# Cross-attention block: rows of x of batch one loaded behind batch zero's transposes, their layer norm in the first group, encoder's rows ahead of the Q products

## The chip, the cores and the metric

The kernel runs on one NeuronCore of one Trainium2 chip. The time is device microseconds of one execution. Before the change the median of three timed runs is 824.66 us (823.79 to 824.75). One more execution was recorded by the hardware profiler; all rows of the profile come from that one.

A core has five engines with queues of their own: TensorE (PE, its weight loads PEld), VectorE (DVE), ScalarE (ACT), GpSimd (POOL) and SyncE (SP), which here only issues transfers. An engine works through its instructions in the order of the program. If one waits, everything behind it waits too.

## The reference

Four batches, each with 512 rows of x and 512 rows of an encoder, 512 features, 16 heads of 32 features. All in float32.

```python
x = layer_norm(hidden_states, ln1_w, ln1_b)
q = x @ q_w + q_b ; k = enc @ k_w + k_b ; v = enc @ v_w + v_b     # 16 heads of 32
scores = einsum('bhqd,bhkd->bhqk', q, k) / sqrt(32)               # masked
out = softmax(scores) @ v
hidden = out @ cproj_w + cproj_b + hidden_states
y = layer_norm(hidden, ln2_w, ln2_b)
y = gelu(y @ fc_w + fc_b) @ proj_w + proj_b                       # 512 -> 2048 -> 512
return hidden + y
```

## The kernel before

**Groups.** The heads are worked in groups of four: 16 groups `w` = 0 to 15, four to a batch. In this text a group is named by this number. For each group there is a K product, a Q product and a V product (`prep_k`, `prep_q`, `prep_v`; lines 191 to 226): each is a chain of matmuls into one of four accumulators (`acc_tile`), which ScalarE then copies out with its bias. GpSimd adds the bias of V (`v_bias`, L230). After its last matmul each product issues the load of the same weight for two groups later (`load_w`, L189).

**Scores.** A group has four score tiles (`scores`, line 233), one for each 128 queries. TensorE writes four heads into one PSUM tile `sc`, of which there is only one: the next score tile can start when VectorE has read all four heads (L245, which also finds the row's extreme `mn`). ScalarE takes the exponential (L249). VectorE then transposes the four heads in blocks of 32 (L277) into a buffer `tb`. After two score tiles (a half, also called a pair below) it adds the reciprocals of the sums (L282 to L285), and SyncE exchanges blocks between partitions with 16 transfers (`copies`, L319) into `pT`, `gt` or `xe`. Then TensorE can multiply by V (`attend`, L362) and VectorE writes the output `oT` (L367). The very first half, of group 0, is instead transposed on TensorE (L263, with copies by VectorE L266 and ScalarE L268).

**Order.** The order is written out by hand. Every group has a list `first[w]` of work with costs, of which `run` puts a share after each score tile, so that TensorE has products between the scores. `AT` and `LAG` say after which score tile each pair is attended: the second half of group 0 before the fourth score tile of group 1, the first half of group 1 before the second score tile of group 2.

**Layer norm of x.** `inputs(b)` returns the pieces for batch `b`: `x1` loads four row tiles (`load_x`, L155), `x2` is three pieces of `ln1` (statistics of row tiles 0 and 1, L116 and L117; statistics of 2 and 3, followed by GpSimd's power `rs`, L122 and L124; normalisation of all four, L128), `x3` four turns, and `x4` loads the encoder's rows (`load_enc`, L150). A turn (`ln_turn`, line 132) transposes one slice of 128 features on TensorE and copies it out with weight and bias, on VectorE (L140) or ScalarE (L142). The turned rows `xT` and the encoder's rows `eT` of a batch lie in one buffer `xe`: the encoder's rows of batch one can be loaded only when the last K or V product of batch zero (group 3) has read those of batch zero.

**SyncE's queue.** Nearly all loads and exchanges are issued by SyncE in program order. A load whose buffer is still in use, and an exchange whose `tb` isn't finished, holds up all that is behind it. An issue also waits until the eighth transfer before it has landed.

**The start.** Loads of weights, encoder and rows of batch zero, then eight weights of the MLP, four row tiles for the residual and the output projection's weight are queued at once; then follow K and V of group 0, K of group 1, four turns, Q of group 0.

Of the kernel before, what the change touches and what calls it, by code (L numbers as in the profile page):

```python
# [74 lines left out]
def xattn_block(ctx: ExitStack, tc: tile.TileContext, x, encT, mask, q_w, k_w, v_w, c_w, fc_w, p_w, vecs, rows, out):  # L75
# [32 lines left out]
    def acc_tile(name):  # L108
        return ps_acc.tile([P, D], F32, tag="acc", name=name)
# [22 lines left out]
    def ln_turn(key, d, xn, dst):  # L132

        w, bi = (LN1W, LN1B) if key[0] == 1 else (LN2W, LN2B)
        tp = acc_tile(f"tp{key[0]}_{key[1]}_{d}")
        for t in range(NT):
            nc.tensor.transpose(tp[:, ts(t, P)], xn[t][:, ts(d, P)], ident)
        wd, bd = vec[:, w + d : w + d + 1], vec[:, bi + d : bi + d + 1]
        if d % 2:
            nc.vector.tensor_scalar(dst[:, d, :], tp, wd, bd, ALU.mult, ALU.add)  # L140
        else:
            nc.scalar.activation(dst[:, d, :], tp, AF.Identity, bias=bd, scale=wd)  # L142


    def queue(b):
        return Q[0] if b else nc.sync

    def load_enc(b):
        for d in range(ND):
            queue(b).dma_start(out=eT[:, d, :], in_=encT[b, ts(d, P), :])  # L150

    def load_x(b):
        S["xn", b] = [tiles.tile([P, D], F32, tag="xn", name=f"xn1_{b}_{t}") for t in range(NT)]
        for t in range(NT):
            queue(b).dma_start(out=S["xn", b][t], in_=x[b, ts(t, P), :])  # L155

    def ln1(b, part):

        xn = S["xn", b]
        for t in range(NT):  # L160
            if part == 2:
                ln_norm((1, b), t, xn[t], xn[t])
            elif t // 2 == part:
                ln_stat((1, b), t, xn[t])
        if part == 1:
            ln_rs((1, b))

    def ln1_turn(b, d):
        ln_turn((1, b), d, S["xn", b], xT)

    def load_mask(b, queue):
        queue.dma_start(out=m8, in_=mask[b : b + 1, :].broadcast_to([P, L]))

    def make_mb(b):
        mb = one.tile([P, L], F32, tag="mb", name=f"mb_{b}")
        nc.vector.tensor_scalar(mb, m8, 0.0, FMAX, ALU.is_equal, ALU.mult)
        if b + 1 < B:
            load_mask(b + 1, nc.gpsimd)
        S["mb", b] = mb

    def load_w(w, queue=None, names=("wk", "wq", "wv")):

        if w >= NW:
            return
        g = w % NG
        for n, src in (("wk", k_w), ("wq", q_w), ("wv", v_w)):
            if n in names:
                S[n, w] = two.tile([P, ND, P], F32, tag=n, name=f"{n}_{w}")
                (queue or Q[0]).dma_start(out=S[n, w], in_=src[:, g, :, :])  # L189

    def prep_k(w):
        b, g = divmod(w, NG)
        kT = kqp.tile([P, L], F32, tag="kT", name=f"kT_{w}")
        acc = acc_tile(f"acck_{w}")
        for d in range(ND):
            nc.tensor.matmul(acc, S["wk", w][:, d, :], eT[:, d, :], start=(d == 0), stop=(d == ND - 1))  # L196
        load_w(w + 2, names=("wk",))
        nc.scalar.activation(kT, acc, AF.Identity, bias=vec[:, KB + g : KB + g + 1], scale=1.0)
        S["kT", w] = kT

    def prep_q(w):
        b, g = divmod(w, NG)
        qT = kqp.tile([P, L], F32, tag="qT", name=f"qT_{w}")
        acc = acc_tile(f"accq_{w}")
        for d in range(ND):
            nc.tensor.matmul(acc, S["wq", w][:, d, :], xT[:, d, :], start=(d == 0), stop=(d == ND - 1))  # L206
        load_w(w + 2, names=("wq",))

        nc.scalar.activation(qT, acc, AF.Identity, bias=qb[:, g : g + 1], scale=-scale)
        S["qT", w] = qT  # L210

    def prep_v(w):
        b = w // NG
        v = five.tile([P, NT, P], F32, tag="v", name=f"v_{w}")
        acc = acc_tile(f"accv_{w}")
        for t in range(NT):
            for d in range(ND):
                nc.tensor.matmul(  # L218
                    acc[:, ts(t, P)], eT[:, d, ts(t, P)], S["wv", w][:, d, :],
                    start=(d == 0), stop=(d == ND - 1),  # L220
                )
        load_w(w + 2, names=("wv",))
        nc.scalar.copy(v, acc.rearrange("p (t f) -> p t f", t=NT))  # L223
        S["v", w] = v
        if w:
            v_bias(w)

    def v_bias(w):
        v, bias = S["v", w], row[:, 2, ts(w % NG, P)]
        nc.gpsimd.tensor_tensor(v, v, bias[:, None, :].broadcast_to([P, NT, P]), ALU.add)  # L230
# [185 lines left out]
    def norm2(b, t):  # L416
        h = S["h", b, t]
        y = tiles.tile([P, D], F32, tag="xn", name=f"xn2_{b}_{t}") if stays(b, t) else h
        S.setdefault(("yn", b), {})[t] = y
        ln_norm((2, b), t, y, h)  # L420

    def proj_bias(b):
        for t in range(NT):
            if stays(b, t):
                add_row(S["hid", b, t], 1)

    def ln2_turn(b, d):
        if d == 0:
            S["yT", b] = keep.tile([P, ND, L], F32, tag="yT", name=f"yT_{b}")
        ln_turn((2, b), d, S["yn", b], S["yT", b])  # L430
# [264 lines left out]
    CHAIN, TURN = 3.4, 0.5  # L695

    def do(fn):
        return [(0.0, fn)]

    def A(w):  # L700
        if w >= NW:
            return []
        return [
            (CHAIN, lambda: prep_k(w)),
            (CHAIN, lambda: prep_q(w)),
            (CHAIN, lambda: prep_v(w)),
        ]

    def C(b):
        return [(CHAIN, lambda t=t: cproj(b, t)) for t in range(NT)]  # L710

    def turns1(b):
        return [(TURN, lambda d=d: ln1_turn(b, d)) for d in range(ND)]

    def turns2(b):
        return [(TURN, lambda d=d: ln2_turn(b, d)) for d in range(ND)]
# [7 lines left out]
    def inputs(b):  # L724
        ln = [(0.0, lambda part=part: ln1(b, part)) for part in range(3)]
        return do(lambda: load_x(b)), ln, turns1(b), do(lambda: load_enc(b))

    def run(work, budget=None):

        spent = 0.0  # L730
        while work and (budget is None or spent + work[0][0] / 2 <= budget):
            cost, fn = work.pop(0)
            fn()
            spent += cost
        return spent
# [26 lines left out]
    prep_v(0)  # L762
    prep_k(1)
    run(turns1(0))
    make_mb(0)
    nc.vector.tensor_scalar(qb, vec[:, QB : QB + NG], 0.0, -scale, ALU.add, ALU.mult)
    prep_q(0)
# [2 lines left out]

    first = [[] for _ in range(NW)]
    later = [[] for _ in range(NW)]
    x1, x2, x3, x4 = inputs(1)
    k2, q2, v2 = A(2)
    k3, q3, v3 = A(3)
    k4, q4, v4 = A(4)
    first[0] = [(CHAIN, lambda: prep_v(1)), (CHAIN, lambda: prep_q(1))] + x1 + [k2, q2]
    first[1] = x2[:1] + [v2, k3] + x2[1:2] + [v3] + x4 + x2[2:] + [q3]
    first[2] = x3[:2] + [k4] + x3[2:] + [v4, q4] + A(5)[:1]
    first[3] = A(5)[1:] + A(6)  # L780
    mlp = []
    for p in range(NORMAL):
# [2 lines left out]
    def some(n):  # L785
        taken, mlp[:n] = mlp[:n], []
        return taken
# [10 lines left out]
    def pb_(b):  # L798
        return do(lambda: proj_bias(b))
# [7 lines left out]
    def norm(b, *ts_):  # L807
        return do(lambda: [norm2(b, t) for t in ts_])


    x1, x2, x3, x4 = inputs(2)
    first[3] = x1 + first[3] + cb(0)
    k, q, v = A(7)
    c, t2 = C(0), turns2(0)
    first[4] = [k] + x2[:1] + [q] + x2[1:2] + [v] + x4 + x2[2:]
    later[4] = c[:1] + x3[:2] + c[1:2] + x3[2:] + c[2:] + stat(0, 0, 1, 2, 3) + rs(0)
    k, q, v = A(8)
    first[5] = norm(0, 0, 1, 2, 3) + [q, k] + t2[:2] + [v] + t2[2:] + pb_(0) + some(5)
    k, q, v = A(9)
    x1, x2, x3, x4 = inputs(3)  # L820
    first[6] = [k, q] + some(5) + [v] + x1
    k, q, v = A(10)
    first[7] = [k, q] + x2[:1] + some(3) + x2[1:2] + some(3) + [v]

    k, q, v = A(11)
    first[8] = h_(1, 0, 1) + x2[2:] + [k, q] + x3[:2] + some(1) + x3[2:] + [v] + h_(1, 2, 3) + x4
    later[8] = cb(1) + C(1)
    k, q, v = A(12)
    first[9] = [q] + some(2) + [k] + some(3) + [v]
    k, q, v = A(13)  # L830
    first[10] = [k, q] + some(5) + [v]
    k, q, v = A(14)
    t2 = turns2(1)
# [3 lines left out]
    k, q, v = A(15)  # L837
# [99 lines left out]
```

## Time and profile before

| what | value |
|---|---|
| median of three timed runs | 824.66 us (823.79 to 824.75) |
| profiled execution | 822.63 us |
| its span, first to last instruction | 820.5 us |
| around the span | 2.1 us |
| TensorE busy | 803.1 us, 98% |
| VectorE busy | 563.1 us, 69% |
| ScalarE busy | 348.0 us, 42% |
| GpSimd busy | 90.6 us, 11% |
| mean granted TensorE clock | 0.998 |

Each row of a timeline gives the start and the length in us, the engine, the line of the program, the operation, what it writes and reads, and in brackets how long the engine sat idle before it and what released it. Consecutive instructions of one kind are merged and counted (x8). TensorE does a float32 matmul in two passes, so a chain of four shows as x8. The stretches give, for windows of the span, how long each engine was busy, the granted TensorE clock (1.00 is full), the share of DMA engines in use and GB/s. "To landing" is the time from the start of a transfer's issue until its data has landed.

### The profile page before, as it was taken

To read this page: it belongs to the slowest core of one execution; us is meant where nothing else is said; L and a number is where in the kernel's file an instruction comes from. 1 tells how busy PE (TensorE), PEld (TensorE's weight loads), DVE (VectorE), ACT (ScalarE), POOL (GpSimd) and SP (SyncE) were. 2 spreads that over 40 slices of the span, in tenths; PEclk is the share of its full clock that TensorE was granted. 3 is DMA by queue.
4 is the path that set the end of the run, shared out by engine and by line. 5 is a ranking of instruction groups with operands and counts; after the bars stand their busy time and mean duration, and the time that the engine had idled before them with its cause. 6 is when DMAs were issued, how large, how long until landed. Compare 5 with 4: busy or idle time off the path is not lost.

```text
span 820.5 us, 11894 instructions
## 1 busy us (share of the span) xinstructions
PE 803.1 (98%) x4020; PEld 465.9 (57%) x4020; DVE 563.1 (69%) x1264; ACT 348.0 (42%) x741; POOL 90.6 (11%) x98
## 2 busy tenths in 40 slices
PE   9996999999999999999999999999999999999998
PEld 6552545444454554454544444444447888888887
DVE  3698889986576778667886767787327986368511
ACT  2655555356654744465436367556202331023200
POOL 1001003111000111000111210010201012200011
PEclk9999999999999999999999999999999999999999
DMA  9668789756668768678677676877734550023001
GB/s 328 235 150 241 184 240 252 191 148 161 168 160 231 179 169 238 159 207 200 155 205 190 164 194 159 199 174 184 205 116 166 191 169 14 26 78 90 2 13 39
DMA packets 59740, 134.91 MB, mean 164 GB/s; under 512 B 12144, under 2 KB 14320, under 8 KB 59552
## 3 DMA queue, kind: packets, MB, share of 16 engines
q1 hardware_dynamic: 58416, 130.73, 58.8%
q0 software_dynamic: 736, 2.29, 0.8%
q10 hardware_dynamic: 528, 1.14, 0.6%
q8 instruction: 32, 0.52, 0.3%
q14 instruction: 28, 0.23, 0.1%
HBM read 58.74 MB, written 6.29 MB: 79 GB/s over the span
## 4 chain that ended last, share of the span: by engine, by line
PE 91%; DVE 5%; SPq 2%; DMA 1%; issue 1%; ACT 0%; POOL 0%; DVEq 0%; POOLq 0%; ACTq 0%
PE accp L467 14%; PE accf L457 14%; PE q L561 12%; PE sc L240 8%; PE av L362 7%; PE accc L399 6%; PE acck L196 6%; PE accv L218 6%; PE accq L206 6%; DVE s L245 2%; PE q4p L601 2%; PE q3p L601 2%; PE q7p L601 2%; PE q6p L601 2%; PE q2p L601 2%; PE q1p L601 2%
## 5 line engine op out<-in xcount | busy, mean ns | idle before, releaser
L249 ACT ACTIVATE s<-s,mn 128x512 f32<-128x512 f32 x256 | 181.6, 711 | 139.6 <-DVE mn L245 139.3
L245 DVE CUSTOM_DVE_ANT_0 s<-sc,mb 128x512 f32<-128x512 f32 x256 | 161.3, 686 | 53.8 <-PE sc L240 53.7
L277 DVE STREAM_TRANSPOSE tb<-s 128x512 f32<-128x512 f32 x248 | 161.6, 690 | 8.5 <-ACT s L249 8.5
L457 PE MATMUL accf<-yT,fcw 128*128 128x512 f32 x256 | 115.5, 599 | 1.5 <-DVE yT L140 1.5
L467 PE MATMUL accp<-pw,gt 128*128 128x512 f32 x256 | 115.0, 598 | 0.0
L457 PEld LDWEIGHTS accf<-yT,fcw 128*128 128x128 f32 x256 | 47.2, 190 | 66.5 <-issue 55.9
L467 PEld LDWEIGHTS accp<-pw,gt 128*128 128x128 f32 x256 | 47.2, 190 | 63.8 <-issue 61.1
L240 PE MATMUL sc<-kT,qT 32*128 32x512 f32 x512 | 73.0, 640 | 4.6 <-DVE mn L245 3.8
L218 PEld LDWEIGHTS accv<-wv,xe 128*128 128x128 f32 x512 | 58.7, 192 | 9.0 <-issue 6.5
L196 PE MATMUL acck<-xe,wk 128*128 128x512 f32 x128 | 60.3, 615 | 3.2 <-DMA xe<-encT_dram 3.2
L218 PE MATMUL accv<-wv,xe 128*128 128x128 f32 x512 | 60.8, 277 | 0.7 <-ACT xe L142 0.4
L561 PE MATMUL q<-ys,gt 128*128 128x256 f32 x256 | 60.1, 379 | 0.0
L206 PE MATMUL accq<-xe,wq 128*128 128x512 f32 x128 | 58.5, 600 | 0.0
L399 PE MATMUL accc<-wc,oT 128*128 128x512 f32 x128 | 56.9, 597 | 0.0
L362 PE MATMUL av<-pT,v 128*32 128x256 f32 x864 | 52.2, 382 | 1.7 <-DMA wv<-v_w_dram 1.7
L561 PEld LDWEIGHTS q<-ys,gt 128*128 128x128 f32 x256 | 48.6, 190 | 6.6
L249 ACT ACT_TABLE_LOAD x22 | 28.2, 1283 | 52.7 <-DVE mn L245 52.7
L230 POOL TENSOR_TENSOR v<-v,row 128x512 f32<-128x512 f32 x16 | 20.3, 1270 | 264.3 <-ACT v L223 264.3
L249 ACT ACTIVATION_READ_ACCUMULATOR s<-s,mn 128x1 f32 x256 | 47.8, 187 | 0.0
L561 PE MATMUL q<-yT,gt 128*128 128x256 f32 x192 | 46.3, 379 | 0.0
L196 PEld LDWEIGHTS acck<-xe,wk 128*128 128x128 f32 x128 | 23.8, 195 | 36.0 <-issue 31.2
L362 PEld LDWEIGHTS av<-pT,v 128*32 128x32 f32 x864 | 25.5, 109 | 30.3 <-issue 11.9
(117 smaller groups left out, 841.5 us busy)
## 6 DMA issues: line engine op xcount, KB each, us to landing
pT<-tb SPq DMA_DIRECT2D x416, 136.0 KB, 2.4
fcw<-fc_w_dram SPq DMA_DIRECT2D x32, 256.0 KB, 3.1
pw<-p_w_dram SPq DMA_DIRECT2D x32, 256.0 KB, 3.5
gt<-fc_w_dram SPq DMA_DIRECT2D x32, 256.0 KB, 2.8
gt<-tb SPq DMA_DIRECT2D x48, 136.0 KB, 2.4
wk<-k_w_dram SPq DMA_DIRECT2D x16, 256.0 KB, 3.4
xe<-encT_dram SPq DMA_DIRECT2D x16, 256.0 KB, 5.2
wv<-v_w_dram SPq DMA_DIRECT2D x16, 256.0 KB, 3.2
```

The costliest lines, as they stand in the source:

```text
L196: nc.tensor.matmul(acc, S["wk", w][:, d, :], eT[:, d, :], start=(d == 0), stop=(d == ND - 1))
L206: nc.tensor.matmul(acc, S["wq", w][:, d, :], xT[:, d, :], start=(d == 0), stop=(d == ND - 1))
L218: nc.tensor.matmul(acc[:, ts(t, P)], eT[:, d, ts(t, P)], S["wv", w][:, d, :], start=(d == 0), stop=(d == ND - 1),)
L240: nc.tensor.matmul(sc[:, h, :], qT[r, ts(qt, P)], kT[r, :], start=True, stop=True)
L245: nc.vector.tensor_tensor_reduce(out=s, in0=sc[:, h, :], in1=S["mb", w // NG], scale=1.0, scalar=FMAX, op0=ALU.add, op1=ALU.min, accum_out=mn,
L249: nc.scalar.activation(s, s, AF.Exp, bias=mn, scale=-1.0, accum_out=sums[:, qt, h : h + 1])
L277: nc.vector.transpose(tv[:, q, h], S["ps", w, qt][h])
L362: nc.tensor.matmul(av[ts(h, HD), : 2 * P].rearrange(shape, **kw), v[:, t, ts(h, HD)], p[t][h], start=(t == 0), stop=(t == NT - 1),)
L399: nc.tensor.matmul(acc, S["oT", b][:, g, ts(t, P)], wc[:, g, :], start=(g == 0), stop=(g == NG - 1))
L457: nc.tensor.matmul(acc, S["fcw", b, f][:, d, :], S["yT", b][:, d, :], start=(d == 0), stop=(d == ND - 1))
L467: nc.tensor.matmul(acc, gT[q % 2][:, k, ts(t, P)], S["pw", b, q * FQ + k], start=(k == 0), stop=(k == FQ - 1))
L561: nc.tensor.matmul(o, a[:, k], y[:, k], start=(k == 0), stop=(k == 1))
```

## The change

Four things are moved, and nothing is computed that wasn't computed before.

- The four row tiles of x of batch one are loaded right behind the turns of batch zero, ahead of the Q product of group 0, no longer in the middle of group 0.
- The layer norm of batch one, three pieces, is placed into group 0 (before: the statistics in group 1, the normalisation before the last product of group 1). Two of its turns come at the end of group 1 instead of the beginning of group 2.
- The products of groups 1 to 3 are put in another order: K of group 3 and V of group 2 move into group 0, Q of group 2 into group 1. V of group 3 is the first product of group 1, and the load of the encoder's rows of batch one is issued right behind it, ahead of Q of groups 2 and 3. Before, it was issued behind V of group 3 too, but later in group 1.
- In every `ln_turn`, of both layer norms and all batches, slices 1 and 2 are copied by VectorE and slices 0 and 3 by ScalarE; before, 1 and 3 by VectorE, 0 and 2 by ScalarE. In group 5 three turns instead of two stand before the V product.

```diff
@@ ln_turn @@
-        if d % 2:
+        if d in (1, 2):
             nc.vector.tensor_scalar(dst[:, d, :], tp, wd, bd, ALU.mult, ALU.add)
         else:
             nc.scalar.activation(dst[:, d, :], tp, AF.Identity, bias=bd, scale=wd)
@@ the start @@
     run(turns1(0))
+    x1, x2, x3, x4 = inputs(1)
+    run(x1)
     make_mb(0)
...
     prep_q(0)
...
-    x1, x2, x3, x4 = inputs(1)
...
-    first[0] = [(CHAIN, lambda: prep_v(1)), (CHAIN, lambda: prep_q(1))] + x1 + [k2, q2]
-    first[1] = x2[:1] + [v2, k3] + x2[1:2] + [v3] + x4 + x2[2:] + [q3]
-    first[2] = x3[:2] + [k4] + x3[2:] + [v4, q4] + A(5)[:1]
+    first[0] = [(CHAIN, lambda: prep_v(1))] + x2[:1] + [(CHAIN, lambda: prep_q(1))] + x2[1:2] + [k2] + x2[2:] + [k3, v2]
+    first[1] = [(CHAIN, lambda: (prep_v(3), load_enc(1)))] + [q2, q3] + x3[:2]
+    first[2] = [k4] + x3[2:] + [v4, q4] + A(5)[:1]
...
-    first[5] = norm(0, 0, 1, 2, 3) + [q, k] + t2[:2] + [v] + t2[2:] + pb_(0) + some(5)
+    first[5] = norm(0, 0, 1, 2, 3) + [q, k] + t2[:3] + [v] + t2[3:] + pb_(0) + some(5)
```

The instructions of the two kernels are the same in number and kind. On VectorE the first two statistics stand right behind the two copies of the first transposed score tile, the other two behind the reciprocals of that half, and the normalisation between the transposes of the third score tile and the reading of the fourth. On TensorE the K products of groups 2 and 3 stand before the third and fourth score tile of group 0.

## The prediction

> **What bounds the kernel now.** TensorE is busy 803.1 of 820.5 us, so a change can win only what TensorE waits for or runs at a lowered clock. I read first the waits of TensorE (who waited for whom: total us, times, longest):
>
> ```profile
> PE sc L240 <- DVE mn L245: 3.8, 3, 2.7
> PE acck L196 <- DMA xe<-encT_dram: 3.2, 1, 3.2
> PE av L362 <- DMA wv<-v_w_dram: 1.7, 1, 1.7
> PE accf L457 <- DVE yT L140: 1.5, 1, 1.5
> ```
>
> The first two, 7.0 us, lie close together. The timeline of TensorE (start, length, idle before and its releaser) puts them in groups 1 and 2:
>
> ```profile
> 56.53 1.14 PE L240 MATMUL sc<-kT,qT 32*128 32x512 f32 x8 [0.60 <-DVE mn L245]
> 61.37 1.93 PE L362 MATMUL av<-pT,v 128*32 128x256 f32 x32
> 63.83 1.14 PE L240 MATMUL sc<-kT,qT 32*128 32x512 f32 x8 [0.52 <-DVE mn L245]
> 71.26 1.14 PE L240 MATMUL sc<-kT,qT 32*128 32x512 f32 x8 [2.66 <-DVE mn L245]
> 76.66 5.36 PE L196 MATMUL acck<-xe,wk 128*128 128x512 f32 x8 [3.23 <-DMA xe<-encT_dram]
> ```
>
> The last row also takes 5.36 us where other K products take 3.70. The stretches of 1 us say why (columns: stretch, its length, five busy times, granted clock, DMA share, GB/s):
>
> ```profile
> 72.00:73.00 1.00, 1.00 (x10) 0.67 (x7) 1.00 (x3) 0.97 (x3) 0.00 (x0) 1.00 0.73 235
> 75.00:76.00 1.00, 0.00 (x0) 0.00 (x0) 1.00 (x5) 0.82 (x3) 0.00 (x0) 1.00 0.81 289
> 78.00:79.00 1.00, 1.00 (x2) 0.34 (x1) 1.00 (x3) 0.78 (x3) 0.00 (x0) 0.50 1.02 278
> 80.00:81.00 1.00, 1.00 (x4) 0.39 (x3) 0.02 (x1) 0.00 (x0) 0.00 (x0) 0.97 1.00 244
> ```
>
> After the 3.2 us wait the clock is 0.50 from about 76.6 to 80.0. So some 8.7 us are at stake between 56 and 82: 7.0 of waiting and 1.7 of clock. VectorE is the engine behind group 1: it runs from 47.5 to 80 without a pause, layer norm included:
>
> ```profile
> 29.71 0.69 DVE L245 CUSTOM_DVE_ANT_0 s<-sc,mb 128x512 f32<-128x512 f32 x1 [0.52 <-PE sc L240]
> 52.40 0.65 DVE L116 BATCH_NORM_STATS2 st<-xn 128x6 f32<-128x512 f32 x1
> 66.10 2.33 DVE L128 TENSOR_SCALAR xn<-xn,mv,rs 128x512 f32<-128x512 f32 x4
> ```
>
> Last, SyncE's queue. One exchange of a pair is 16 issues in 10.4 us, and all wait in one line with the loads:
>
> ```profile
> 22.23 1.00 SPq L189 DMA_DIRECT2D wq<-q_w_dram  x1
> 33.61 1.81 SPq L155 DMA_DIRECT2D xn<-x_dram  x4
> 46.80 10.43 SPq L319 DMA_DIRECT2D pT<-tb  x16
> 72.13 1.85 SPq L150 DMA_DIRECT2D xe<-encT_dram  x4
> ```
>
> **The change, step by step.** I walk the new order with durations of before, on its clock. A score tile costs VectorE 2.45 us (four L245), its transposes 2.41, the end of a half (L282 to L285) 0.97; TensorE takes 1.07 for scores, 3.63 for a K or Q product, 3.77 for V, 1.86 for an attend.
>
> *1. Rows of x.* The four loads move from 33.6 to the place of the Q weight issued at 22.2, past three weight loads (Q of group 2, V and Q of group 3); these come later but are wanted only at about 51 to 70. The place is in the start-up backlog, with 390 GB/s moving. For the Q weight in that place the trace shows
>
> ```profile
> L189 SPq DMA_DIRECT2D wq<-q_w_dram x1: 997/997/997, 22.2 to 22.2; - x1
> DMA to landing us min/median/max: 8.4/8.4/8.4
> ```
>
> that is 22.2 + 8.4 = 30.6. The loads before it land at 28.7, 29.4 and 30.0 (8.5, 8.5, 8.4 after issue), 0.65 apart, so I put the rows at 30.6, 31.3, 31.9, 32.6. The Trainium skill (DMA: Bandwidth & Descriptors, section on the anatomy of one DMA) fits 2.0 us plus bytes over 436 GB/s, stated for the GpSimd path: 256 KB give 2.6 us and a landing near 25, before VectorE asks. I take the row: it is this queue, loaded. By the rule the sum below would be about 1.4 us better.
>
> *2. Statistics in group 0.* VectorE is free at 29.2, but L116 of row tiles 0 and 1 stand ahead of the next four L245. They wait for the landings, end at about 32.15, and L245 starts there instead of at 29.71: 2.4 late. Behind it are the exponentials (ScalarE ends 35.7 instead of 33.3), then the copy of Q (36.3), whose accumulator the fourth transpose needs, then ScalarE's copy of the first transpose (36.9), whose accumulator the next K product needs. That product starts at 36.95 instead of about 34.9: TensorE loses 2.0.
>
> *3. Two K products ahead of scores.* K of group 2 now stands before the third score tile and K of group 3 before the fourth. Scores end at 41.7; VectorE starts them at 41.8 instead of 36.05. Statistics 2 and 3 (1.58) and GpSimd's power (1.5) fit in before. Then 2.45 + 2.41 to 46.65, the four L128 (1.85, no GpSimd beside them) to 48.5, 2.42 + 2.40 + 0.97 to 54.3, plus 0.3 because L284 falls beside GpSimd's V bias: 54.6. Before, this half was done at 46.8.
>
> *4. Its exchange* therefore runs 54.65 to 65.1 and lands at 64.5 + 2.4 = 66.9 (2.4 us is the row of the last issues). Before it landed at 59.0 and the attend at 61.37 did not wait.
>
> *5. TensorE in between.* K 40.6, scores 41.7, K 45.3, scores 46.4, V 50.1, row sums and attend 52.2, scores 53.3, V 57.0; scores wait for VectorE until 57.5 and end 58.6; Q 62.2; scores 63.45. Then the attend waits for the exchange: 3.45 us. It ends 68.8, scores 69.85, Q 73.5, two turns 74.5, scores 75.6.
>
> *6. The encoder.* Its issues follow the exchange and two V weights: 66.0 to 67.9, landing 70.4 to 73.1 (4.4 to 5.7 after issue). K of group 4 asks at 75.6 and doesn't wait: the 3.2 us and their clock are gone. But the next exchange starts 1.9 later for it: 67.9 to 78.3, landed 80.2. TensorE has done K and a turn at 79.7, waits 0.5, attends to 82.1, scores 83.2, turn 83.7, V 87.35.
>
> *7. The sum.* That V product ended at 89.55 before: 2.2 us gained. From here both orders are alike, TensorE has no idle time until 141, and later exchanges land 0.9 or more before their attends, so the gain stays.
>
> *8. The clock.* The new wait of 3.45 us can halve the clock too. The Trainium skill (TensorE: Matmul & The Clock Gate, Part 1) says the clock halves after a whole idle window of 3.4 us, windows running free. A 3.45 us wait hardly ever holds a whole one, so by the rule nothing is lost. The rows above are stricter: 3.2 us were enough, while 2.66 us just before were not. I take the row: 1.7 lost, of which the 0.5 wait of step 6 is absorbed, so 1.2. Gain left: 1.0.
>
> *9. Turns.* Feature slices 1 and 2 go to VectorE, 0 and 3 to ScalarE, all through: no instruction more. In batch zero the Q product reaches slice 2 at 19.2, after VectorE's second turn (18.4). In batch two and three the copies land beside waits of another cause. These I cost at 0, hidden by TensorE's queue of products; without cover each is at most 0.8, one L140. In group 5, though, the wait at L457 (1.5) ends on VectorE, where
>
> ```profile
> 182.31 1.21 DVE L284 COPY rr<-rsum 128x256 f32<-128x256 f32 x1
> ```
>
> takes 1.21 instead of 0.29, ending just after GpSimd's V bias (182.10 to 183.36). A third turn now stands before that V product (0.44), so the bias starts near 182.55 and L284 may be through at 182.60: 0.9 gained. If it is caught all the same, 0.4 lost. I take 0.9.
>
> Sum: 1.0 + 0.9 = 1.9 us off the profiled execution's 822.63 (820.5 span and 2.1 around it), 820.7. The timed median is 824.66, 2.0 above it; I take the difference over: 822.8.
>
> **The rivals.** *A, the cover holds.* The rows land before 29.2, or the clock stays. Without the wait of step 2 VectorE reaches 40.4 instead of 41.8 and the whole walk is 0.9 to 1.4 better; with the clock kept, 1.2 more. For it: the free-running window. Against: 390 GB/s in the rows up to 28. Time: 824.66 - 4.0 = 820.6.
> *B, slower: the exchange of step 4 takes the place of the waits removed.* Everything that delays VectorE between 30 and 54 goes one for one through the exchange into the attend at 63.45. For it: before, that attend had 2.4 us to spare, and now it has less than none. The 1.9 us are used up when it lands after 68.8, 1.9 later than I have it. Rows of x landing 1.9 later do it; at 3.9 later the time is 822.8 + 3.9 = 826.7.
> *C, no change.* The clock is halved and L284 is caught: 1.0 - 0.4 = 0.6 gained, 824.1.
>
> **How the numbers follow.** Mine 0.45, A 0.17, B 0.23, C 0.15. Within 0.2%, 1.65 us, a measurement of this kernel can't tell a change. Mine lies at 1.9 with an uncertainty of about 1.2, so 0.29 of its 0.45 are faster and 0.16 the same; A is faster; B slower by more than 1.65 in 0.20; C the same. Faster 0.47, same 0.33, slower 0.20. The range goes from a little under A, 820.2, to B at 826.7.
>
> **What would show it.** Right: no wait of L196 for the encoder near 75; a wait of about 3.5 us of L362 for an exchange near 63 to 67, with the clock at 0.50 for some 3 us behind it; L116 waiting for x until about 30.6 and 31.3; 2 us lost in short waits from 33 to 37; L284 near 182 at 0.29. Wrong: rows of x that land at 26 or after 33; the attend not waiting; a wait after 90 that before didn't have.

## The result and the profile after

The changed kernel took 824.97 us (median of 12 runs, 822.91 to 827.83), the kernel before in the same series 824.93 us (12 runs, 823.79 to 828.24): ratio 0.9995, 95% interval 0.9981 to 1.0009, so between 1.6 us faster and 0.7 us slower. The forecast of 1.9 us gained did not come; no change is what was measured. The profiled execution took 823.17 us with a span of 821.4.

The waits of TensorE in the changed kernel (who waited for whom: total us, times, longest):

```profile
PE av L362 <- DMA pT<-tb: 6.7, 2, 3.4
PE accv L218 <- ACT xe L142: 0.9, 1, 0.9
PE accv L218 <- ACT yT L142: 0.9, 1, 0.9
PE av L362 <- DMA gt<-tb: 0.4, 1, 0.4
PE accf L457 <- DVE yT L140: 0.2, 1, 0.2
```

The waits that headed the list before are gone: 3.8 us for VectorE before scores, 3.2 for the encoder, 1.5 at L457. In their place stand two waits, 3.3 and 3.4 us, of an attend for its exchange. The timeline of TensorE shows where:

```profile
57.47 1.14 PE L240 MATMUL sc<-kT,qT 32*128 32x512 f32 x8 [0.30 <-DVE mn L245]
66.78 3.64 PE L362 MATMUL av<-pT,v 128*32 128x256 f32 x32 [3.34 <-DMA pT<-tb]
70.35 1.96 PE L240 MATMUL sc<-kT,qT 32*128 32x512 f32 x8
77.81 3.70 PE L196 MATMUL acck<-xe,wk 128*128 128x512 f32 x8
82.39 1.93 PE L362 MATMUL av<-gt,v 128*32 128x256 f32 x32 [0.45 <-DMA gt<-tb]
145.31 1.93 PE L362 MATMUL av<-pT,v 128*32 128x256 f32 x32 [3.40 <-DMA pT<-tb]
```

The K product of group 4 (77.81) no longer waits for the encoder and takes its normal 3.70. The attend of pair 1 (66.78) waits 3.34 us, and it and the scores behind it run at half speed: 3.64 in place of 1.93, 1.96 in place of 1.14. Stretches of 3.41 us of the changed kernel (stretch, length, five busy times with TensorE's first, granted clock, DMA share, GB/s) show the clock at half from 65.2 to 72.0:

```profile
61.80:65.22 3.42, 1.58 (x10) 0.31 (x8) 3.35 (x9) 2.20 (x7) 0.00 (x0) 1.00 0.97 222
65.22:68.63 3.41, 1.85 (x20) 1.07 (x24) 3.41 (x11) 2.41 (x7) 0.00 (x0) 0.50 0.85 247
68.63:72.04 3.41, 3.41 (x28) 1.02 (x20) 2.15 (x4) 0.51 (x2) 0.00 (x0) 0.50 1.02 343
```

The attend of pair 7 (145.31) is the second loser. Before, it stood like this:

```profile
143.65 1.93 PE L362 MATMUL av<-pT,v 128*32 128x256 f32 x32 [1.75 <-DMA wv<-v_w_dram]
```

Where does one execution stand against the other? The first K product took 4.52 us after and 3.60 before, and the first transposes of batch zero began at 16.71 against 15.68. The change has nothing ahead of them; in the runs below that product takes between 3.60 and 4.73, so it goes with the execution. The table gives both readings, by the time in the span and counted from those transposes (us that the changed kernel is ahead):

| at | in the span | from the transposes |
|---|---|---|
| V product of group 4 ends | 0.0 | 1.0 |
| V product before pair 7's attend starts | 0.0 | 1.0 |
| pair 7's attend starts | -1.7 | -0.6 |
| scores at 157 | -0.7 | 0.3 |
| attend at 187, behind L457 | 0.2 | 1.2 |
| last product | -0.9 | 0.1 |

Up to pair 1's exchange the first reading is the better one, since the walk there hangs on the landing of x, which does not move with TensorE's start: in two runs below the transposes began 1.28 and 0.92 us earlier than here, and pair 1's exchange only 0.38 and 0.21. So nothing was won by 90, 1.7 us were lost at 145, 0.9 came back by 157 (transposes and a wait for L400 that no longer lie in the way), 0.9 at L457, and 1.1 went in two waits of the V product for ScalarE's turns, near 299 and 429. Single executions of either kernel differ by 4 to 5 us, so that these two end 0.9 apart goes with equal medians.

### The profile page after: what moved, and what is told of

Its sections match the earlier page's. It is cut to its first block, busy times and chain, and to the rows that moved or that the text cites. A ratio compares the mean times of both kernels' runs of the same rounds, so it can differ in the third digit from the quotient of the medians.

```text
span 821.4 us, 11900 instructions
## 1 busy us (share of the span) xinstructions
PE 805.0 (98%) x4020; PEld 467.0 (57%) x4020; DVE 562.7 (69%) x1264; ACT 347.7 (42%) x741; POOL 90.4 (11%) x98
## 3 DMA queue, kind: packets, MB, share of 16 engines
q10 hardware_dynamic: 528, 1.14, 0.5%
## 4 chain that ended last, share of the span: by engine, by line
PE 85%; DMA 5%; DVE 5%; SPq 3%; issue 1%; ACT 1%; DVEq 0%; ACTq 0%
PE accp L467 14%; PE accf L457 14%; PE q L561 12%; PE sc L240 7%; PE accc L399 7%; PE av L362 6%; PE accv L218 4%; PE acck L196 4%; PE accq L206 4%; SPq L319 3%; PE q4p L601 2%; PE q3p L601 2%; PE q7p L601 2%; PE q2p L601 2%; PE q5p L601 2%; PE q6p L601 2%
## 5 line engine op out<-in xcount | busy, mean ns | idle before, releaser
L245 DVE CUSTOM_DVE_ANT_0 s<-sc,mb 128x512 f32<-128x512 f32 x256 | 161.3, 686 | 55.4 <-PE sc L240 55.2
L457 PE MATMUL accf<-yT,fcw 128*128 128x512 f32 x256 | 115.5, 599 | 0.5 <-ACT v L223 0.3
L457 PEld LDWEIGHTS accf<-yT,fcw 128*128 128x128 f32 x256 | 47.2, 190 | 65.5 <-issue 55.5
L362 PE MATMUL av<-pT,v 128*32 128x256 f32 x864 | 53.9, 391 | 6.7 <-DMA pT<-tb 6.7
L367 DVE TENSOR_TENSOR oT<-av,pT 128x256 f32<-128x256 f32 x26 | 11.0, 422 | 46.7 <-PE av L362 43.9
```

Source lines behind the costliest of these rows:

```text
L245: nc.vector.tensor_tensor_reduce(out=s, in0=sc[:, h, :], in1=S["mb", w // NG], scale=1.0, scalar=FMAX, op0=ALU.add, op1=ALU.min, accum_out=mn,
L362: nc.tensor.matmul(av[ts(h, HD), : 2 * P].rearrange(shape, **kw), v[:, t, ts(h, HD)], p[t][h], start=(t == 0), stop=(t == NT - 1),)
L457: nc.tensor.matmul(acc, S["fcw", b, f][:, d, :], S["yT", b][:, d, :], start=(d == 0), stop=(d == ND - 1))
```

## The experiments

**The two halves of the change.** First the mapping of the turns alone, on the kernel before:

```
-        if d % 2:
+        if d in (1, 2):
...
-    first[5] = norm(0, 0, 1, 2, 3) + [q, k] + t2[:2] + [v] + t2[2:] + pb_(0) + some(5)
+    first[5] = norm(0, 0, 1, 2, 3) + [q, k] + t2[:3] + [v] + t2[3:] + pb_(0) + some(5)
```

> The kernel before with the eviction mapping of the transposes (slices 1 and 2 on VectorE) and the third turn of group 5 alone; all loads and products as before. Theory T (the late exchange of pair 1, the halved clock behind it and the backlog of SyncE that reaches pair 7 ate the gain): the mapping is worth nearly nothing, 1.1 us gained at L457 in group 5 (wait 1.54 becomes 0.3 to 0.5), 0.4 lost at the V product near 299 and 0.65 at the one near 429: within 0.3 us of the kernel before; attend of pair 1 and of pair 7 wait as before (0 and 1.7). Rival M (the mapping ate the gain): at least 1 us slower than the kernel before.

823.92 us against 824.01: ratio 0.9998 (0.9982 to 1.0015). The three places came out as expected; from TensorE's waits in this kernel:

```profile
PE av L362 <- DMA wv<-v_w_dram: 2.8, 1, 2.8
PE accv L218 <- ACT xe L142: 0.9, 1, 0.9
PE accv L218 <- ACT yT L142: 0.9, 1, 0.9
PE accf L457 <- DVE yT L140: 0.2, 1, 0.2
```

The gain at L457 and the losses at the two V products cancel. Pair 7 waited 2.8 us here, against 1.75 before, though nothing ahead of it but the mapping had changed; whether the mapping or the execution made that 1.0 us is open.

Then the moves alone: the changed kernel with both edits above undone.

> The changed kernel with the mapping of the kernel before (slices 1 and 3 on VectorE, two turns ahead of V in group 5). T: pair 1's attend still waits 3.3 us and is halved in clock for 6 us or more, pair 7's still waits 3.4; L457 in group 5 waits 1.5 again, V products near 299 and 429 wait 0.4 and 0.2: within 0.3 us of the changed kernel. M: at least 1 us faster than the changed kernel.

825.45 us: ratio 1.0014 (0.9997 to 1.0031), no difference from the kernel before or the changed one that the interval can settle. The waits are as expected: 1.5 at L457, and

```profile
66.38 3.38 PE L362 MATMUL av<-pT,v 128*32 128x256 f32 x32 [3.33 <-DMA pT<-tb]
69.69 1.14 PE L240 MATMUL sc<-kT,qT 32*128 32x512 f32 x8
145.83 3.64 PE L362 MATMUL av<-pT,v 128*32 128x256 f32 x32 [3.77 <-DMA wv<-v_w_dram]
```

Pair 1's attend waits as in the changed kernel (3.33 and 3.34), but here half speed ends with it, after 3.4 us and not 6 or more: 1.45 us lost instead of 2.5. At pair 7 it is the other way round. So half speed behind the same wait costs differently; why, the part on step 8 shows.

**Pair 1's exchange.** Is it late because VectorE's work stands ahead of it? The normalisation of batch one's rows was moved out of the way:

```
-    first[0] = ... + x2[1:2] + [k2] + x2[2:] + [k3, v2]
-    first[1] = [(CHAIN, lambda: (prep_v(3), load_enc(1)))] + [q2, q3] + x3[:2]
+    first[0] = ... + x2[1:2] + [k2, k3, v2]
+    first[1] = [(CHAIN, lambda: (prep_v(3), load_enc(1)))] + x2[2:] + [q2, q3] + x3[:2]
```

> The changed kernel with the normalisation of batch one's rows (four L90) moved from behind K of group 2 in group 0 to behind V of group 3 in group 1. T: VectorE reaches the second score tiles 1.2 to 1.8 us earlier, pair 1's exchange lands near 65.0, its attend waits 1.5 to 2.1; clock gate either not tripped (then 3.5 to 4 us ahead at the V product of group 4) or as in the changed kernel (1.5 ahead). Q products of group 1 must not wait for the later transposes by over 1 us. Rival X: no change.

824.08 us: ratio 0.9999 (0.9984 to 1.0014). (The normalisation is the four L128; L90 in the expectation is a slip.) The exchange began at 52.61, 2.07 us earlier than in the changed kernel, TensorE came 0.77 earlier, and the attend waited 1.22 less, 2.12 us: what VectorE saves here comes off TensorE's wait one for one, less the 0.77. Rival X, that nothing changes there, falls. But the saving was spent at once, in TensorE's timeline of this run:

```profile
64.78 2.86 PE L362 MATMUL av<-pT,v 128*32 128x256 f32 x32 [2.12 <-DMA pT<-tb]
68.16 2.09 PE L240 MATMUL sc<-kT,qT 32*128 32x512 f32 x8 [0.51 <-DVE mn L245]
70.18 4.82 PE L206 MATMUL accq<-xe,wq 128*128 128x512 f32 x8
144.39 3.47 PE L362 MATMUL av<-pT,v 128*32 128x256 f32 x32 [3.52 <-DMA wv<-v_w_dram]
```

Three operations at half speed cost 0.9, 0.95 and 1.1 us, more than behind the longer wait. Pair 7's attend began 0.9 us earlier than in the changed kernel and lost 1.5 of it again by half speed.

The V product of group 2 was taken out of VectorE's and TensorE's way as well, in two versions. In the first it landed behind the load of batch one's encoder rows, so V of group 2 is there computed from batch one's rows and not from batch zero's:

```
-    first[0] = ... + [k3, v2]
-    first[1] = [(CHAIN, lambda: (prep_v(3), load_enc(1)))] + [q2, q3] + x3[:2]
+    first[0] = ... + [k3]
+    first[1] = [(CHAIN, lambda: (prep_v(3), load_enc(1)))] + [v2, q2, q3] + x3[:2]
```

> The changed kernel with one product moved: V of group 2 goes from the end of group 0 to the start of group 1. Two K products then still stand ahead of the third score tile's turn, but not the V product. T: pair 1's half is done near 52.5 in place of 54.7, its exchange has landed near 64.9, TensorE asks for it near 65: wait under 0.5 us, no slice at half clock, V product of group 4 ends near 85 to 86 (89.5 in the changed kernel). What of these 4 us reaches the end depends on pair 7: if its exchange stays where it is, its wait grows from 3.4 to 5 or more and the gain at the end is 1 to 2 us; if it moves along, 3 to 4 us. Rival X (the landing of x at 30.6 and VectorE behind it set the loss): no change.

835.21 us, ratio 1.0133 (1.0100 to 1.0166). It says nothing on either theory: the V product waited 12.2 us for the encoder rows. The second version puts it ahead of that load:

```
+    first[1] = [v2] + [(CHAIN, lambda: (prep_v(3), load_enc(1)))] + [q2, q3] + x3[:2]
```

> The changed kernel with V of group 2 moved from the end of group 0 to the start of group 1, ahead of V of group 3 and of the load of batch one's encoder rows. Theory T: pair 1's half is done 2.5 us earlier, its exchange has landed when TensorE asks for it (wait under 0.7 us, no half clock there), and 4 us are gained at the first product behind it; but SyncE's queue, full from pair 1's exchange to pair 7's, only moves up by these 2.5 us, so pair 7's attend waits longer than the 3.4 us of the changed kernel, 4.5 to 5.5, and 2 to 3 us are gained at the end. Rival V (VectorE's work, not the queue, sets pair 7): pair 7 waits as before, 4 us gained at the end.

828.37 us, ratio 1.0037 (1.0023 to 1.0052): slower. From TensorE's timeline:

```profile
64.85 1.93 PE L362 MATMUL av<-pT,v 128*32 128x256 f32 x32
78.64 6.54 PE L196 MATMUL acck<-xe,wk 128*128 128x512 f32 x8 [5.21 <-DMA xe<-encT_dram]
```

Pair 1's attend waits for nothing and keeps its clock, as expected. But the encoder's issues, which follow V of group 3, now come behind the second exchange in SyncE's line, at 74.92 instead of 65.96, and the K product waits 5.21 us and runs at half speed for 2.8 more. The wait that the change had removed is back, larger. At pair 1 T's mechanism held; its sum did not, because this queue was left out of it. At pair 7 T and V both missed: the attend waited 2.58 us, neither 4.5 to 5.5 nor the 3.40 of the changed kernel.

**Pair 7: queue or transfers?** My theory was that SyncE's queue, full of issues from pair 1's exchange on, keeps pair 7's exchange back. In the changed kernel VectorE finished pair 7's half at 129.7, and SyncE started its exchange at 132.72:

```profile
115.28 1.87 SPq L155 DMA_DIRECT2D xn<-x_dram  x4
117.73 13.28 SPq L319 DMA_DIRECT2D gt<-tb  x16
132.72 10.29 SPq L319 DMA_DIRECT2D pT<-tb  x16
```

So the weights' issues were given to another engine, first to GpSimd:

```
-                (queue or Q[0]).dma_start(out=S[n, w], in_=src[:, g, :, :])
+                (queue or (nc.gpsimd if 2 <= w < 10 else Q[0])).dma_start(out=S[n, w], in_=src[:, g, :, :])
```

> The changed kernel with the loads of the K, Q and V weights of groups 2 to 9 issued by GpSimd instead of SyncE: 12 issues with their gaps, some 6.7 us, leave SyncE's queue between pair 1's exchange and pair 7's. T (the queue is full there and sets pair 7): pair 7's exchange starts 4 to 6 us earlier, its attend waits under 0.5 us, 3.4 to 5 us gained over the changed kernel; pair 1's wait of 3.3 stays. Rival V: pair 7's wait stays above 2.5 us and the time within 0.5 us of the changed kernel.

> The kernel before with the same weights issued by GpSimd. T: pair 7's attend, which waited 1.75 us in the profile before and 2.7 in that of the mapping alone, waits under 0.5: 1.5 to 3.5 us faster than before, and less gain than the same edit brings on the changed kernel. Rival V: within 0.5 us of before.

> Both: V of group 2 first in group 1, and the weights of groups 2 to 9 issued by GpSimd. T: neither pair 1 nor pair 7 makes TensorE wait over 0.7 us: 6 to 8 us faster than the changed kernel and than the kernel before. If the gains of the two edits do not add, 3 to 5.

832.23, 829.12 and 836.05 us: ratios 1.0097 (1.0077 to 1.0117), 1.0050 (1.0034 to 1.0066) and 1.0141 (1.0122 to 1.0160). All slower, all expectations missed. VectorE and GpSimd of the changed kernel with this edit show where most of it goes; the other two kernels have the same copy at 5.81 us:

```profile
129.92 1.27 POOL L230 TENSOR_TENSOR v<-v,row 128x512 f32<-128x512 f32 x1
130.42 5.81 DVE L284 COPY rr<-rsum 128x256 f32<-128x256 f32 x1
131.15 4.93 POOL L374 TENSOR_TENSOR h<-h,row 128x512 f32<-128x512 f32 x4
```

A copy that takes 0.29 us alone ended only when GpSimd had ended its V bias and four additions behind it; then pair 7's half was 5 us late. Without the edit the same copy took 0.82, ending with the V bias (it came 0.60 us after the bias began, here 0.50). To test that cause, the four additions were moved behind the next mask's load, which waits for VectorE:

```
-    first[3] = x1 + first[3] + cb(0)
+    first[3] = x1 + first[3]
...
-    first[4] = [k] + x2[:1] + ...
+    first[4] = cb(0) + [k] + x2[:1] + ...
```

> The changed kernel with the weights issued by GpSimd as in the earlier run, and the four additions of the projection's bias to batch zero's rows (L374, 4.9 us on GpSimd) moved from the end of group 3 to the start of group 4, behind the mask's load, where no copy L284 of VectorE meets them. Theory G (the copy L284, held 5.81 us while GpSimd ran its V bias and these additions, was the loss of the earlier run): L284 takes under 1.5 us everywhere, pair 7's half is done 4.5 us earlier, its wait falls from 7.2 to under 3, 5 to 8 us faster than the earlier run. Rival: GpSimd's own issues or the order of the weights were the loss: no more than 1 us faster.

827.32 us, ratio 1.0027 (1.0017 to 1.0038), against 1.0097: 5.8 us faster by the ratios. G holds: L284 took 0.94 and pair 7's wait fell from 7.2 to 3.15, a little short of the "under 3". That this kernel is still 0.27% slower than the one before is not accounted for. What is left answers the question: here SyncE starts pair 7's exchange as soon as VectorE has written its half, and yet TensorE waits 3.15 us.

```profile
132.45 0.94 DVE L284 COPY rr<-rsum 128x256 f32<-128x256 f32 x1
133.93 10.05 SPq L319 DMA_DIRECT2D pT<-tb  x16
149.09 3.64 PE L362 MATMUL av<-pT,v 128*32 128x256 f32 x32 [3.15 <-DMA xe<-encT_dram]
```

The last issue ends at 144.0 and the attend begins 5.1 us later; in the changed kernel 2.3 us later. The queue was free and the transfers were late, though here with loads from GpSimd among them.

The same with ScalarE as the issuer, so that GpSimd is left alone, each load behind the eviction of its product:

```
-        load_w(w + 2, names=("wk",))
         nc.scalar.activation(kT, acc, ...)
+        load_w(w + 2, names=("wk",))
```

> The changed kernel with the weights of groups 2 to 9 issued by ScalarE, each behind the eviction of its own product, so that GpSimd keeps its work and its order (the copy L284 of pair 7's second half took 0.82 us behind the V bias in the changed kernel, and 5.81 us with GpSimd's issues). T (SyncE's queue, full from pair 1's exchange on, sets pair 7): pair 7's exchange starts at VectorE's end near 130 in place of 132.7, its attend waits under 1.2 us instead of 3.4 and loses no clock: 2 to 4 us faster than the changed kernel. Pair 1's wait of 3.3 stays. Rival D (the transfers themselves, not their issue, are what is slow there: the DMA engines were 0.9 busy from 96 to 146): pair 7's wait stays above 2.5 and the time within 1 us of the changed kernel.

> The kernel before with the same edit. T: no K product waits over 2 us for the encoder rows (3.2 before, the two weights ahead of them gone), pair 7's attend waits under 1.2 us: 2 to 5 us faster than before. Rival D: within 1 us of before.

846.12 and 848.28 us: ratios 1.0251 (1.0235 to 1.0267) and 1.0282 (1.0268 to 1.0295). T is refuted: taking the issues off SyncE made both kernels 20 us slower. D said that moving issues gains nothing, but did not foresee a loss. It shows in the exchanges, here two of the changed kernel with the edit:

```profile
86.47 13.17 SPq L319 DMA_DIRECT2D pT<-tb  x16
99.74 12.98 SPq L319 DMA_DIRECT2D gt<-tb  x16
```

With loads in ScalarE's queue as well, the 16 issues of an exchange take 13 to 17 us where they took 10 to 13.3 (only the first, ahead of most of these loads, still takes 10.1 in the changed kernel). Why, these runs do not tell: the DMA engines were busy only 0.7 to 0.8 of most of that time.

Last, bytes and issues both taken away. The weights of groups 4 to 7 are not loaded; these groups multiply by those of groups 2 and 3:

```
             if n in names and 4 <= w < 8:
                 S[n, w] = S[n, w - 2]
             elif n in names:
```

> The changed kernel without the loads of the K, Q and V weights of groups 4 to 7: these groups multiply by the weights of groups 2 and 3 that lie in the two buffers. This leaves out 12 transfers of 256 KB (3 MB), ten of them between pair 1's exchange and pair 7's, and with them both their bytes and their issue on SyncE; every instruction on TensorE, VectorE and ScalarE stays. Theory D, after the runs that moved the issue and gained nothing (the stretch from 55 to 145 is full of transfers, the DMA engines 0.9 busy, and pair 7 comes as late as they are through): each exchange starts when VectorE has written its half, pair 7's near 129.7, it lands within 2.5 us of its last issue, its attend waits under 0.8 us in place of 3.4: 3 to 5 us faster than the changed kernel. Pair 1's wait of 3.3 stays. Rival V (VectorE's half of pair 7 comes too late for TensorE whatever the transfers do): pair 7's wait stays above 2 us, gain under 1.5 us.

821.48 us against 825.33: ratio 0.9954 (0.9940 to 0.9967), 3.8 us faster than the kernel before, from which the changed kernel doesn't differ. Rows of SyncE, then of TensorE, lines counted two higher here because of the edit:

```profile
114.14 11.03 SPq L321 DMA_DIRECT2D gt<-tb  x16
128.09 10.07 SPq L321 DMA_DIRECT2D pT<-tb  x16
```

```profile
66.49 3.41 PE L364 MATMUL av<-pT,v 128*32 128x256 f32 x32 [3.27 <-DMA pT<-tb]
141.55 1.93 PE L364 MATMUL av<-pT,v 128*32 128x256 f32 x32 [1.34 <-ACT v L225]
```

Pair 1 waits 3.27 as without this edit; two of the 12 loads stood ahead of it, and they do not make it late. Pair 7 waits 1.34 instead of 3.40, and the 0.45 of the attend near 82 is gone. (The profile names ScalarE's copy as the releaser, but it had ended at 140.9; the last issue of the exchange, at 137.54, took 3.8 us to land, to 141.4.) Rival V falls on both of its numbers. D's bound of 0.8 was too low: the exchange starts when VectorE has written its half (128.03), but its last issue landed after 3.8 us where D counted on 2.5. Of the 3.4 us some 2.1 go with these 12 loads. How much is their issue and how much their bytes, this run can't tell: both were taken away.

## Why the prediction was right and wrong

*Steps 1 to 5 held almost to the tenth, step 6 in part.* In the rows of VectorE and SyncE of the changed kernel:

```profile
30.60 0.69 DVE L116 BATCH_NORM_STATS2 st<-xn 128x6 f32<-128x512 f32 x1 [0.38 <-DMA xn<-x_dram]
32.24 0.69 DVE L245 CUSTOM_DVE_ANT_0 s<-sc,mb 128x512 f32<-128x512 f32 x1
54.68 10.12 SPq L319 DMA_DIRECT2D pT<-tb  x16
65.96 2.14 SPq L150 DMA_DIRECT2D xe<-encT_dram  x4
68.22 12.27 SPq L319 DMA_DIRECT2D gt<-tb  x16
```

Forecast were 30.6 for the rows, 32.15 for L245, 54.65 for the exchange, 66.0 for the encoder, waits of 3.45 and 0.5 for the two attends; measured 3.34 and 0.45. That the 0.45 came out is luck. The exchange behind the encoder took 12.27 us where step 6 counted 10.4, since two of the encoder's loads took 6.8 and 7.1 us to land and not 5.7 at most; it landed at 82.3 and not at 80.2, and TensorE came about as much later. The row of the loaded queue was right about the landing, the 2.0 us plus bytes of the page cited there was not. TensorE's start 1.0 us later took nothing from this: it shortened VectorE's wait for x by as much.

*Step 7 failed: "later exchanges land 0.9 or more before their attends, so the gain stays".* The trace before shows at 143.65 an attend that already waited 1.75 us for its exchange, and the first fence of the prediction lists it; a gain ahead of it would have needed an earlier exchange. It became a later one. VectorE had written the half at 129.7 in both profiles; the exchange began at 130.70 before and at 132.72 after. From the moment VectorE had written that half, the runs show:

| run | us to the attend | of these, until the exchange began |
|---|---|---|
| kernel before | 13.9 | 1.0 |
| mapping alone | 14.9 | 1.2 |
| changed kernel | 15.6 | 3.0 |
| moves alone | 16.0 | 3.2 |
| normalisation later | 15.7 | 2.5 |
| V of group 2 behind the encoder's load | 14.0 | 1.5 |
| V of group 2 first in group 1 | 14.8 | 2.3 |
| without weights of groups 4 to 7 | 13.5 | 0.1 |

With the moves and all loads on SyncE the exchange begins 1.5 to 3.2 us behind VectorE, without the moves 1.0 and 1.2. The stretches of 10 us of the kernel before (DMA share second to last):

```profile
86.00:96.00 10.00, 10.00 (x80) 6.04 (x79) 9.93 (x26) 7.50 (x19) 1.27 (x1) 1.00 0.54 139
116.00:126.00 10.00, 10.00 (x80) 5.47 (x73) 8.00 (x22) 5.74 (x15) 0.00 (x0) 1.00 0.98 288
```

and of the changed kernel:

```profile
46.00:56.00 10.00, 10.00 (x105) 7.74 (x98) 9.86 (x25) 3.80 (x11) 1.27 (x1) 1.00 0.10 30
86.00:96.00 10.00, 10.00 (x80) 6.06 (x79) 9.93 (x25) 6.74 (x17) 1.26 (x1) 1.00 0.91 234
116.00:126.00 10.00, 10.00 (x80) 5.45 (x73) 7.99 (x22) 5.73 (x15) 0.00 (x0) 1.00 0.90 252
```

Before, the exchange of pair 1 ran from 46.8, and there was slack near 90. In the changed kernel next to nothing moves until 54.7, and from then on the share is 0.86 to 0.96 up to 146. It looks as if the pause of step 4 were missing as transfer time 80 us later, but SyncE's rows of these two profiles do not bear that out: the exchange ahead of pair 7's began at 117.72 in the kernel before and at 117.73 in the changed one, so its queue had made the pause up by then. Nor has the mapping alone a pause, and it has 1.0 of the 1.7 us. The 2.0 us arose inside that exchange (13.28 us where it took 11.28), and they begin with one load of x ahead of it, the third of batch two's four, issued at 116.2 in both kernels. From its issue to its landing, in the kernel before and in the changed one:

```profile
DMA to landing us min/median/max: 4.3/4.3/4.3
DMA to landing us min/median/max: 6.4/6.4/6.4
```

It landed at 122.60, and an issue waits until the eighth transfer before it has landed: the exchange's sixth issue began at 122.62, after a gap of 1.8 us, and the next two at 123.86 and 125.25, as the two loads behind it landed at 123.85 and 125.24. With the moves alone that load took 5.4 us, and there the exchange itself began 1.7 us later, at 119.43. So three things stand: the attend of pair 7 waited before already, the load traffic of groups 4 to 7 is some 2.1 of its 3.4 us, and in these single executions the moves go with a later exchange there. By what the moves delay it, and how much of the 1.7 us was that one execution, is open.

*Step 8 was right that the clock halves, and mis-sized: 1.7 us lost in the forecast, of which 0.5 were to be absorbed by the next attend's wait, 2.5 in the profile with 0.45 of that wait left.* TensorE came to the next attend at 81.94, some 0.5 later than the forecast had it with its 1.7; and because the exchange landed late as well, the 0.45 came on top. Together they are the 1.0 us which step 8 had still left and the profile has not. More telling is the spread. Behind waits at the same attend:

| run | wait | half speed | lost to it |
|---|---|---|---|
| changed kernel | 3.34 | 65.2 to 72.0 | 2.5 |
| moves alone | 3.33 | 66.0 to 69.4 | 1.45 |
| without weights of groups 4 to 7 | 3.27 | 66.8 to 70.2 | 1.6 |
| normalisation later | 2.12 | 65.6 to 72.5 | 3.0 |

Half speed lasts 3.41 us or a multiple of it, and what is lost is about half of the time TensorE works in it. And the 2.66 us wait for VectorE that cost nothing in the kernel before cost 1.5 us with the mapping alone. In steps of 3.41 us, laid so that the changes of the clock fall on their borders, the kernel before (first two rows) and the mapping alone (last two) show why:

```profile
66.40:69.81 3.41, 2.20 (x6) 0.65 (x4) 3.41 (x8) 0.35 (x1) 0.38 (x1) 1.00 0.94 217
69.81:73.23 3.42, 1.97 (x16) 1.17 (x16) 3.42 (x10) 3.16 (x9) 0.00 (x0) 1.00 0.89 231
68.60:72.01 3.41, 1.01 (x3) 0.18 (x1) 3.41 (x10) 1.54 (x5) 0.00 (x0) 1.00 0.93 215
72.01:75.42 3.41, 3.15 (x14) 1.65 (x15) 3.34 (x9) 1.97 (x5) 0.00 (x0) 0.50 0.86 239
```

Before, the wait fell on two steps, with TensorE idle for 1.2 and 1.45 us, and nothing followed. With the mapping alone one step had 2.4 us idle, and the next ran at half speed. All fourteen traces agree (counted from 20 us on): of the steps at full speed, all 26 with 2.1 us or more idle were followed by half speed, none of some 3200 with 1.7 or less; of the 7 in between, 3 were. A step at half speed was followed by another when TensorE was idle for 0.9 us or more of it, and never at 0.4 or less. In the changed kernel the end of the wait lay in such a step (1.56 us idle, second row of its stretches above), and so a second one followed; with the moves alone it was 0.4. So the price of a wait hangs on where it falls in these steps, which the walk could not know: that it was 2.5 here and not 1.45 is chance. The page weighed there (TensorE: Matmul & The Clock Gate, Part 1) has windows of that length, running free, and these rows agree; its whole idle window is not needed, 2.12 us of 3.41 were enough.

*Step 9:* the 0.9 at L457 came (1.54 became 0.29 and 0.19). The zero for batches two and three was wrong by 0.44 and 0.65 us at the V products near 299 and 429, where slice 3 is now ScalarE's and ends later; the bound of 0.8 each, given there, holds.

*The sum*, from the profile, in the span: 0.0 up to the V product of group 4 (forecast 1.0), -1.7 at pair 7 (0), +0.9 behind it (0), +0.9 at L457 (0.9), -1.1 at the turns (0): -1.0, and -0.9 is read at the end (forecast 1.9). That 824.97 lies in the range of 820.2 to 826.7 is owed to the width of the range: a gain of 1.0 by 90 was forecast and none was there. Of the rivals, no change came out, but not by its mechanism: L284 near 182 was not caught. B's mechanism is there, nearly one for one with the normalisation moved, but the rows of x came as forecast, so it had nothing to carry.

## What to carry to other kernels

A wait for a transfer that stands further on in the list is a barrier: a gain ahead of it counts only if that transfer moves as well, so follow each gain to the next such wait before adding it up. Delaying an exchange costs at its own consumer first; look also whether the transfers behind it have slack to catch up. And before an issue is moved to a quieter engine, ask what that engine's own work will then collide with. The clock's price for a wait of 2 to 3.5 us belongs in a forecast as a range, here 0 to 3 us, and not as one number.

## What was not expected of the hardware

A VectorE copy of 128x256 fp32 in SBUF (L284) took 0.29 us alone, 0.57 to 1.3 when GpSimd's V bias ran, and 5.81 when the bias was followed by four more additions. The Trainium skill (SBUF — State Buffer, section on SBUF's two separate sides) says that VectorE and GpSimd share a port pair as an exclusive lock held for a whole instruction; here the copy waited through five. Where it paid 5.81, in three kernels, it came 0.50 us after the bias began; where it paid 0.82 with an addition behind the bias, 0.60. Whether that 0.1 us decides was not tried.

With loads in ScalarE's queue the exchanges in SyncE's took some 3 us longer each, and the kernels 20 us in all, at a DMA share below 1. And half speed cost between 0 and 3.0 us behind waits of 2.1 to 3.4: it goes by fixed steps of 3.41 us and by how much of one TensorE was idle, somewhere between 1.7 and 2.1 us, not by the length of the wait.
